# Edge masks from GpSimd to VectorE and the per-node scalar chain from VectorE to GpSimd, in a two-layer graph kernel

## The chip, the cores and the metric

The kernel runs on one core of a Trainium2 chip. Times are device microseconds (us) of one execution. I call the engines as the profile does: PE is TensorE, DVE is VectorE, ACT is ScalarE, POOL is GpSimd. Every kernel ran in turn with the kernel before on the same chip, and its ratio is to that kernel; the experiments used several chips, so two of them are compared by their ratios. A run is called slow when it takes over 1.5% more than the fastest of its kernel; ratios use the other runs, the fast ones.

## The reference, cut to what matters

Two graph layers over 3327 nodes with 64 features and a dense 0/1 adjacency. Layer 0 is an attention in hyperbolic space: a logarithm map for every pair of nodes, a weighted sum over the neighbours, then a chain of per-node steps (a norm, a tanh, a Möbius addition, a projection, a layer norm). Layer 1 weighs each neighbour by 0.5 to the power of its rank from the end of the row.

```python
# layer 0
adj_att = sigmoid(left[:, None] + right[None, :] + b_att[0]) * adj
x_local = logmap(x[:, None, :], x[None, :, :], c)           # every pair
support_t = einsum('ij,ijd->id', adj_att, x_local)
h0 = proj(expmap(x, support_t, c), c)                       # per node: norms, tanh, mobius_add
# ... x = x + h0; layer norm, relu ...
# layer 1
mask = (adj != 0)
rank = cumsum(mask, axis=1); deg = rank[:, -1:]
k = minimum(deg, 100.0);     pos = rank - (deg - k)
w = mask * where(pos > 0, 0.5 ** (k - pos), 0.0)
out = w @ (input @ weight) + bias
```

## The kernel before

The nodes are padded to 26 blocks of 128. The pair stage goes through four strips of columns (8, 8, 6 and 4 blocks wide), with 26, 26, 26 and 13 rounds: a round takes one block of rows (two in the last strip) against the strip. Each round:

- POOL makes an edge mask of the adjacency tile. PE counts edges with it, and ACT or DVE *reads* the count into 8 bits, which layer 1 decodes later.
- PE makes the pair products `pq`. ACT runs two Gelus on them and a tanh for the attention. DVE makes two products: the first with the adjacency, the second with `pq`. PE sums the result.

When a strip has ended, its per-node chain (`post`) is woven into the rounds of the next strip. It is a generator that yields the weight of each portion, and each round takes portions up to a budget. The last strip has no next one: its chain is woven into the decoding of layer 1, which I call the tail.

```python
ON_ACT = ((1, 5), (4, 7), (2, 3), (1, 2))        # share of reads on ACT, by strip
PORTIONS, LAST = (2, 5, 5, 16), 6
BIG, LATER = 4, 99
...
def rsqrt(pool, y, v, n, power=False):
    ...
    if power:
        G.tensor_tensor(y, v, nhalf[:, :n], op=ALU.pow)
        V.tensor_scalar(g, v, -0.5, None, op0=ALU.mult)
        yield LATER
    ...                                          # then Newton steps on DVE
...
def post(agg, b0, nb):
    ...
    A.activation(k, t0, AF.Tanh)
    yield LATER
    V.scalar_tensor_tensor(k, k, absr, rn, op0=ALU.mult, op1=ALU.mult)
    yield 1
    V.tensor_mul(y2, u2, k)
    yield 1
    ...                                          # about 30 more of this kind, 8 columns each
    V.tensor_mul(w, hs, wide(t0, nb))            # 512 columns
    yield BIG
    ...
def edges(n):
    ...
    G.tensor_scalar(*args, 0.0, None, op0=ALU.is_equal)

def read(n, j):
    ...
    rest = none[:, NB - 1 - j : NB - j]
    ...
        A.activation(kept, S.pc[:, : S.F], AF.Relu, bias=rest)
    else:
        V.tensor_scalar(kept, S.pc[:, : S.F], rest, 0.0, op0=ALU.add, op1=ALU.max)

def advance(portions):
    while portions > 0:
        portions -= next(steps, LATER)
...
# inside a round
V.scalar_tensor_tensor(sg, sg, 1.0, ad_of.pop(n)[:, :w], op0=ALU.add, op1=ALU.mult)   # first product
...
if n + 1 < R:
    products(n + 1)
advance(PORTIONS[k])
...
V.scalar_tensor_tensor(sg, pq, WD, sg, op0=ALU.add, op1=ALU.mult)                     # second product
```

Of the kernel before, what the change touches and what calls it, by code (L numbers as in the profile page):

```python
# [34 lines left out]
ON_ACT = ((1, 5), (4, 7), (2, 3), (1, 2))  # L35

PORTIONS, LAST = (2, 5, 5, 16), 6
BIG, LATER = 4, 99
# [403 lines left out]
def fast(ctx, tc, x, adj_t, r, w_att, b_att, weight, bias, out, flag):  # L442
# [35 lines left out]
    G.memset(nhalf, -0.5)  # L478
    ident = const.tile([P, P], F32, name="ident")
# [4 lines left out]

    cb = const.tile([P, P], BF16, name="cb")
    ca = const.tile([P, P], BF16, name="ca")
    G.memset(ca, 1.0)
    G.affine_select(out=cb, in_=ca, compare_op=ALU.is_gt, fill=0.0, base=0,
                    pattern=[[-1, P]], channel_multiplier=1)
    G.affine_select(out=cb, in_=cb, compare_op=ALU.not_equal, fill=-float(MAX_NEIGH), base=0,  # L490
                    pattern=[[-1, P]], channel_multiplier=1)
    G.tensor_sub(ca, ca, cb)

    none_i = const.tile([P, NB], I32, name="none_i")
    none = const.tile([P, NB], F32, name="none")
    G.iota(none_i, pattern=[[-P, NB]], base=MAX_NEIGH - P + 1, channel_multiplier=1)
    G.tensor_copy(none, none_i)
# [6 lines left out]
    def scalar_col(name):  # L504
        return const.tile([P, 1], F32, name=name)

    inv_r, c_c, sqc, absr, maxnorm, c2_c, m2c, negc, zs_c, za_c, f_c = (
        scalar_col(n) for n in ("inv_r", "c_c", "sqc", "absr", "maxnorm", "c2_c", "m2c", "negc", "zs_c", "za_c",
# [3 lines left out]
    def rsqrt(pool, y, v, n, power=False):  # L512

        t = pool.tile([P, n], F32, name="rs_t")
        g = pool.tile([P, n], F32, name="rs_g")
        if power:
            G.tensor_tensor(y, v, nhalf[:, :n], op=ALU.pow)  # L517
            V.tensor_scalar(g, v, -0.5, None, op0=ALU.mult)
            yield LATER
        else:  # L520
            V.tensor_scalar(t.bitcast(I32), v.bitcast(I32), 1, None, op0=ALU.logical_shift_right)
            V.tensor_scalar(y.bitcast(I32), t.bitcast(I32), -1.0, float(0x5F3759DF), op0=ALU.mult, op1=ALU.add)
            V.tensor_scalar(g, v, -0.5, None, op0=ALU.mult)
            yield 3
        for _ in range(1 if power else 3):
            V.tensor_mul(t, y, y)
            yield 1
            V.tensor_mul(t, t, g)
            yield 1
            V.scalar_tensor_tensor(y, t, 1.5, y, op0=ALU.add, op1=ALU.mult)  # L530
            yield 1
# [22 lines left out]
    with tc.tile_pool(name="pre", bufs=1) as pre:  # L554
# [17 lines left out]
        for _ in rsqrt(pre, y, v, NB):  # L572
            pass
# [58 lines left out]
        for _ in rsqrt(pre, yr, x2c, NB):  # L632
            pass
# [44 lines left out]
        V.tensor_scalar(m2c, c_c, -2.0, None, op0=ALU.mult)  # L678

# [40 lines left out]

    def post(agg, b0, nb):

        pool = post_pool
        bs = slice(b0, b0 + nb)

        def small(name):
            return pool.tile([P, nb], F32, name=name)

        def big(name):
            return pool.tile([P, nb, D], F32, name=name)  # L730

        hs, v, xs = h[:, bs], agg[:, :, :D], x_sb[:, bs]
        sa, t0, t1, k, y2, u2, xy, hv, vv, rn = (
            small(n) for n in ("sa", "t0", "t1", "k", "y2", "u2", "xy", "hv", "vv", "rn"))
        u, w, dt = big("u"), big("w"), big("dt")

        A.activation(u, v, AF.Square)
        V.tensor_mul(dt, hs, v)
        yield BIG
        V.tensor_reduce(hv, dt, AX.X, ALU.add)  # L740
        yield BIG
        V.tensor_reduce(vv, u, AX.X, ALU.add)
        yield BIG
        V.scalar_tensor_tensor(sa, hv, m2c, agg[:, :, D], op0=ALU.mult, op1=ALU.add)
        yield 1
        V.tensor_mul(sa, sa, su[:, bs])
        yield 1

        V.tensor_mul(xy, hv, sv[:, bs])
        yield 1  # L750
        V.tensor_mul(t0, sa, x2[:, bs])
        yield 1
        V.tensor_sub(xy, xy, t0)
        yield 1
        V.tensor_mul(u2, vv, sv[:, bs])
        yield 1
        V.tensor_mul(t0, sa, hv)
        yield 1
        V.tensor_sub(u2, u2, t0)
        yield 1  # L760
        V.tensor_mul(u2, u2, sv[:, bs])
        yield 1
        V.tensor_mul(t0, sa, xy)
        yield 1
        V.tensor_sub(u2, u2, t0)
        yield 1
        V.tensor_scalar(u2, u2, 0.0, None, op0=ALU.max)
        yield 1

        V.tensor_scalar(t0, u2, MIN_NORM, None, op0=ALU.max)  # L770
        yield 1
        yield from rsqrt(pool, rn, t0, nb, True)
        V.tensor_mul(t0, t0, rn)
        yield 1
        V.tensor_mul(t0, t0, sk[:, bs])
        yield 1
        A.activation(k, t0, AF.Tanh)
        yield LATER
        V.scalar_tensor_tensor(k, k, absr, rn, op0=ALU.mult, op1=ALU.mult)
        yield 1  # L780

        V.tensor_mul(y2, u2, k)
        yield 1
        V.tensor_mul(y2, y2, k)
        yield 1
        V.tensor_mul(xy, xy, k)
        yield 1
        V.tensor_scalar(xy, xy, m2c, -1.0, op0=ALU.mult, op1=ALU.mult)
        yield 1
        V.tensor_scalar(xy, xy, 1.0, None, op0=ALU.add)  # L790
        yield 1
        V.scalar_tensor_tensor(t0, y2, c_c, xy, op0=ALU.mult, op1=ALU.add)
        yield 1
        V.scalar_tensor_tensor(t1, y2, c2_c, x2[:, bs], op0=ALU.mult, op1=ALU.mult)
        yield 1
        V.tensor_add(t1, t1, xy)
        yield 1
        V.tensor_scalar(t1, t1, MIN_NORM, None, op0=ALU.max)
        yield 1
        V.reciprocal(t1, t1)  # L800
        yield 1
        V.tensor_mul(k, k, bal[:, bs])
        yield 1
        V.tensor_mul(k, k, t1)
        yield 1
        V.tensor_mul(t0, t0, t1)
        yield 1
        V.tensor_mul(t1, k, sa)
        yield 1
        V.tensor_sub(t0, t0, t1)  # L810
        yield 1
        V.tensor_mul(k, k, sv[:, bs])
        yield 1

        V.tensor_mul(y2, t0, x2[:, bs])
        yield 1
        V.tensor_mul(t1, k, hv)
        yield 1
        V.tensor_add(y2, y2, t1)
        yield 1  # L820
        V.tensor_mul(y2, y2, t0)
        yield 1
        V.tensor_mul(hv, hv, t0)
        yield 1
        V.tensor_mul(vv, vv, k)
        yield 1
        V.tensor_add(vv, vv, hv)
        yield 1
        V.tensor_mul(vv, vv, k)
        yield 1  # L830
        V.tensor_add(y2, y2, vv)
        yield 1
        V.tensor_scalar(y2, y2, MIN_NORM, None, op0=ALU.max)
        yield 1

        yield from rsqrt(pool, rn, y2, nb, True)
        V.tensor_scalar(rn, rn, maxnorm, 1.0, op0=ALU.mult, op1=ALU.min)
        yield 1
        V.tensor_mul(t0, t0, rn)
        yield 1  # L840
        V.tensor_mul(k, k, rn)
        yield 1
        V.tensor_mul(w, hs, wide(t0, nb))
        yield BIG
        V.tensor_mul(u, v, wide(k, nb))
        yield BIG
        V.tensor_add(xs, xs, w)
        yield BIG
        V.tensor_add(xs, xs, u)
        yield BIG  # L850

        V.tensor_reduce(t0, xs, AX.X, ALU.add)
        yield BIG
        V.scalar_tensor_tensor(w, wide(t0, nb), -1.0 / D, xs, op0=ALU.mult, op1=ALU.add)
        yield BIG
        A.activation(dt, w, AF.Square)
        yield LATER
        V.tensor_reduce(t0, dt, AX.X, ALU.add)
        yield BIG
        V.tensor_scalar(t0, t0, 1.0 / D, EPS_LN, op0=ALU.mult, op1=ALU.add)  # L860
        yield 1
        yield from rsqrt(pool, rn, t0, nb, True)
        V.tensor_scalar(rn, rn, HS, None, op0=ALU.mult)
        yield 1
        V.scalar_tensor_tensor(w, w, 0.0, wide(rn, nb), op0=ALU.max, op1=ALU.mult)
        yield BIG
        A.copy(s2[:, bs, 0], w)
        yield LATER
        V.tensor_sub(s2[:, bs, 1], w, s2[:, bs, 0])
        yield BIG  # L870
# [69 lines left out]
    def edges(n):  # L940
        mask_of[n] = mask = work.tile([P, FMAX], BF16, name="mask", bufs=3)
        args = mask[:, : span(n)], ad_of[n][:, : span(n)]

        G.tensor_scalar(*args, 0.0, None, op0=ALU.is_equal)  # L944
# [14 lines left out]
    def read(n, j):  # L959
# [4 lines left out]
        rest = none[:, NB - 1 - j : NB - j]  # L964
        i = NB - 1 - j
        if (n < AHEAD and k == 0) or i * num // den != (i + 1) * num // den:
            A.activation(kept, S.pc[:, : S.F], AF.Relu, bias=rest)  # L967
        else:
            V.tensor_scalar(kept, S.pc[:, : S.F], rest, 0.0, op0=ALU.add, op1=ALU.max)  # L969
# [45 lines left out]

    def advance(portions):
        while portions > 0:
            portions -= next(steps, LATER)
# [11 lines left out]
    with tc.manual_schedule(engines=IN_ORDER):  # L1030
        products(0)
        for n in range(R):
# [20 lines left out]
            elif n == 1:  # L1053
                left_to_dram()
            if turned:
# [13 lines left out]
            if n + 1 < R:  # L1069
                products(n + 1)  # L1070
            advance(PORTIONS[k])
# [3 lines left out]
            if ended:  # L1075
                strip_out(k - 1)
            V.scalar_tensor_tensor(sg, pq, WD, sg, op0=ALU.add, op1=ALU.mult)  # L1077
# [13 lines left out]
    with tc.tile_pool(name="l1", bufs=2, reuse_waits="tile") as l1, \  # L1091
# [22 lines left out]
        for j in range(late):  # L1114
            wt = decode(j)
            advance(LAST)
# [88 lines left out]
```

## Time and profile before

The kernel took 458.52 us (median of three runs, 457.63 to 458.9). The first line of the page gives the busy time of each engine, its share of the span, and how many instructions it ran:

```profile
PE 368.4 (81%) x1460; PEld 155.6 (34%) x1460; DVE 393.1 (86%) x660; ACT 369.9 (81%) x399; POOL 289.7 (63%) x137
```

No engine is full over the whole span, so the averages don't name the bound; it has to be read stage by stage. The prediction below does that. Its stages start where the first Gelu of each strip starts; the tail starts 3.7 us after the first Gelu of the last round. GpSimd's masks take 2.8 us each on average, and DVE instructions that meet one are stretched.

### The profile page before, as it was taken

How to read it: one execution, taken by the hardware profiler on the slowest of the kernel's cores; microseconds unless marked ns; L12 is line 12 of the kernel's file. 1: busy time of each engine (PE TensorE's matmuls, PEld its weight loads, DVE VectorE, ACT ScalarE, POOL GpSimd, SP SyncE). 2: the span in 40 equal slices, each digit the busy share in tenths (PEclk: the TensorE clock that was granted, in tenths of full speed). 3: DMA queues.
4: the chain of work that ended last, by engine and by line, in shares of the span. 5: the costliest groups of instructions: out<-in, count | busy, mean ns of one | idle time of the engine just before them, and what ended most of it. 6: DMA issues, size and time to landing. Idle time of an engine off the chain costs nothing.

```text
span 456.4 us, 4831 instructions
## 1 busy us (share of the span) xinstructions
PE 368.4 (81%) x1460; PEld 155.6 (34%) x1460; DVE 393.1 (86%) x660; ACT 369.9 (81%) x399; POOL 289.7 (63%) x137
## 2 busy tenths in 40 slices
PE   0336799999998989879889988698778689678973
PEld 0034233333333323323334444343332232233453
DVE  4893899999999799998999999999889999789821
ACT  1647989999999899887899999779798689577930
POOL 8910699887897697695968787959877541014000
PEclk9997999999998999998999999989899899999987
DMA  7402455545555343444236444336443100000002
GB/s 201 201 12 62 136 157 170 166 141 155 154 194 157 110 130 105 143 130 138 73 102 182 119 123 136 103 106 175 146 124 102 53 1 0 1 0 1 1 21 62
DMA packets 23313, 48.98 MB, mean 107 GB/s; under 512 B 8713, under 2 KB 9169, under 8 KB 23279
## 3 DMA queue, kind: packets, MB, share of 16 engines
q1 hardware_dynamic: 20993, 47.66, 35.0%
q10 hardware_dynamic: 2062, 0.87, 0.9%
q0 software_dynamic: 224, 0.07, 0.3%
q8 instruction: 13, 0.21, 0.2%
q14 instruction: 21, 0.17, 0.1%
HBM read 46.40 MB, written 0.87 MB: 104 GB/s over the span
## 4 chain that ended last, share of the span: by engine, by line
PE 34%; DVE 32%; ACT 20%; issue 7%; DMA 2%; POOL 2%; DVEq 0%; ACTq 0%; POOLq 0%
PE po L993 14%; DVE sg L1077 8%; DVE sg L1058 7%; ACT pq L1048 4%; PE pq L983 4%; ACT wt L1100 4%; ACT sg L976 4%; PE pq L984 4%; PE pc L956 4%; PE pc L955 4%; ACT pq L1049 3%; PE pw L1107 2%; DVE behind_lo L969 2%; DVE behind_hi L969 2%; DMA w_lr<-in_w_att 2%
## 5 line engine op out<-in xcount | busy, mean ns | idle before, releaser
L944 POOL TENSOR_SCALAR mask<-ad 128x1024 bf16<-128x1024 f32 (+1 forms) x91 | 254.5, 2801 | 81.9 <-PE pc L955 57.8
L993 PE MATMUL po<-sg,hw 128*65 128x512 f32 (+1 forms) x364 | 161.7, 568 | 1.6 <-DVE sg L1077 1.3
L1058 DVE SCALAR_TENSOR_TENSOR sg<-sg,ad 128x1024 f32<-128x1024 f32 (+1 forms) x91 | 112.6, 1237 | 6.6 <-ACT sg L976 6.5
L1077 DVE SCALAR_TENSOR_TENSOR sg<-pq,sg 128x1024 f32<-128x1024 f32 (+1 forms) x91 | 103.8, 1141 | 2.7 <-ACT pq L1049 1.5
L1048 ACT ACTIVATE pq<-pq 128x1024 f32<-128x1024 f32 (+1 forms) x91 | 86.7, 952 | 20.3 <-PE pq L984 14.9
L976 ACT ACTIVATE sg<-left_b,right 128x1024 f32<-128x1024 f32 (+2 forms) x104 | 100.5, 980 | 0.0
L1049 ACT ACTIVATE pq<-pq 128x1024 f32<-128x1024 f32 (+1 forms) x91 | 86.2, 947 | 2.9
L955 PE MATMUL pc<-mask,ca 128*128 128x512 bf16 (+1 forms) x175 | 66.5, 380 | 23.4 <-DVE behind_hi L969 8.3
L983 PE MATMUL pq<-iu,ju 71*128 71x512 f16 (+1 forms) x182 | 68.7, 377 | 17.0 <-DVE sg L1077 16.3
L956 PE MATMUL pc<-mask,cb 128*128 128x512 bf16 (+1 forms) x182 | 67.7, 382 | 12.6 <-POOL mask L944 11.1
L993 PEld LDWEIGHTS po<-sg,hw 128*65 128x65 f32 x364 | 49.9, 139 | 72.8 <-issue 56.4
L984 PE MATMUL pq<-iz,jz 128*128 128x512 f16 (+1 forms) x182 | 67.5, 378 | 3.8 <-DMA iz<-jz 3.8
L1107 PE MATMUL pw<-wt,s 128*128 128x512 bf16 (+1 forms) x182 | 40.4, 371 | 10.2 <-ACT wt L1100 7.0
L956 PEld LDWEIGHTS <-cb 128*128 128x128 bf16 x182 | 18.2, 100 | 74.2 <-issue 54.3
L969 DVE TENSOR_SCALAR behind_hi<-pc,none 128x1024 uint8<-128x1024 f32 (+2 forms) x26 | 28.2, 1084 | 6.9 <-PE pc L956 6.7
L969 DVE TENSOR_SCALAR behind_lo<-pc,none 128x1024 uint8<-128x1024 f32 (+2 forms) x26 | 29.0, 1115 | 5.1 <-ACT pq L1049 2.6
L967 ACT ACTIVATE behind_hi<-pc,none 128x1024 uint8<-128x1024 f32 (+2 forms) x26 | 24.6, 945 | 8.0 <-PE pc L956 7.9
L983 PEld LDWEIGHTS <-ju 71*128 71x128 f16 x182 | 18.3, 100 | 36.8 <-DVE sg L1077 18.0
L967 ACT ACTIVATE behind_lo<-pc,none 128x1024 uint8<-128x1024 f32 (+2 forms) x26 | 23.9, 919 | 7.8 <-PE pc L956 7.8
L517 POOL TENSOR_TENSOR rn<-t,nhalf 128x8 f32<-128x8 f32 (+2 forms) x8 | 13.7, 1709 | 25.1 <-DVE t L770 22.4
L984 PEld LDWEIGHTS <-jz 128*128 128x128 f16 x182 | 18.3, 101 | 31.2 <-issue 12.0
L1107 PEld LDWEIGHTS <-s 128*128 128x128 f16 x182 | 17.8, 100 | 30.3 <-issue 11.6
(227 smaller groups left out, 302.7 us busy)
## 6 DMA issues: line engine op xcount, KB each, us to landing
ad<-in_adj_t SPq DMA_DIRECT2D x65, 512.0 KB, 3.6
ad<-in_adj_t SPq DMA_DIRECT2D x26, 384.0 KB, 3.2
out<-o SPq DMA_DIRECT2D x6, 128.0 KB, 1.9
left_b<-left_d SPq DMA_DIRECT2D x1, 512.0 KB, 4.7
x_sb<-in_x ACTq DMA_DIRECT2D x1, 416.0 KB, 5.7
x_sb<-in_x SPq DMA_DIRECT2D x1, 416.0 KB, 5.0
left_b<-left_d SPq DMA_DIRECT2D x1, 384.0 KB, 4.1
iz<-jz ACTq DMA_DIRECT2D x2, 128.0 KB, 2.3
```

The costliest lines, as they stand in the source:

```text
L944: G.tensor_scalar(*args, 0.0, None, op0=ALU.is_equal)
L955: T.matmul(S.pc[:, f0:f1], ca, S.before[:, f0:f1], start=False, stop=True, skip_group_check=True)
L956: T.matmul(S.pc[:, f0:f1], cb, now[:, f0:f1], start=S.first, stop=True, skip_group_check=True)
L969: V.tensor_scalar(kept, S.pc[:, : S.F], rest, 0.0, op0=ALU.add, op1=ALU.max)
L976: A.activation(part(n, sg, j), S.left[:, : S.F], AF.Tanh, bias=right[:, j : j + 1], scale=0.5)
L983: T.matmul(part(n, pq, j, f0, f1), ju[:KB, j, :], S.iu[:, f0:f1], start=True, stop=False)
L984: T.matmul(part(n, pq, j, f0, f1), jz[:, j, :], S.iz[:, f0:f1], start=False, stop=True)
L993: T.matmul(S.po[: D + 1, f0:f1], hw[:, j, :], part(n, sg_of[n], j, f0, f1), start=j == NB - 1, stop=j == 0)
L1048: A.activation(pq, pq, AF.Gelu, scale=-WG / QS)
L1049: A.activation(pq, pq, AF.Gelu, scale=WH)
L1058: V.scalar_tensor_tensor(sg, sg, 1.0, ad_of.pop(n)[:, :w], op0=ALU.add, op1=ALU.mult)
L1077: V.scalar_tensor_tensor(sg, pq, WD, sg, op0=ALU.add, op1=ALU.mult)
```

## The change

The intent is to relieve DVE in strips 1 to 3 and to keep late work out of the way of the next round's products:

1. Masks go to DVE (`not_equal` in place of `is_equal`, with the signs of the counting matrices turned). The bias column `none` goes from both kinds of read.
2. The small instructions of the chain, for the three hidden strips, are recorded and issued on GpSimd in bursts, each followed by some rounds that are left to it (`after(slots)`: 2, 4 and 2 rounds). Roots and the reciprocal become a power and some small steps.
3. The last strip's chain stays on DVE; its roots become bit-shift roots of 11 instructions instead of GpSimd powers.
4. The portions go behind the second product (in the last hidden strip, strip 3, one of two helpings stays ahead of it), and ACT's steps of the chain come one round later.
5. Shares and budgets are set anew.

```diff
-ON_ACT = ((1, 5), (4, 7), (2, 3), (1, 2))
-PORTIONS, LAST = (2, 5, 5, 16), 6
+ON_ACT = ((1, 2), (5, 8), (3, 4), (1, 2))
+PORTIONS, LAST = (2, 4, 4, 8), 8
...
+    class Asked:                       # records calls instead of issuing them
+        ...
+            return lambda *args, **kwargs: self.to.append((getattr(self.engine, name), args, kwargs))
...
+        hidden = b0 + nb < NB
+        W = Asked(G if hidden else V, asked_of_w)
...
+        def after(slots):
+            for do, args, kwargs in asked_of_w:
+                do(*args, **kwargs)
+                if not hidden:
+                    yield 1
+            asked_of_w.clear()
+            if not hidden:
+                pass
+            elif nb > 6:
+                yield from [LATER] * slots
+            else:
+                yield from [LATER] * (slots + slots // 2)
+
+        def root(y, v):
+            ...
+            if hidden:
+                W.tensor_tensor(y, v, nhalf[:, :nb], op=ALU.pow)
+                ...                     # 4 small steps
+            else:
+                rsqrt(W, pool, y, v, nb)
...
+        yield from after(2)
+        yield ACT
         A.activation(k, t0, AF.Tanh)
-        yield LATER
-        V.scalar_tensor_tensor(k, k, absr, rn, op0=ALU.mult, op1=ALU.mult)
-        yield 1
-        ...
+        yield 0
+        scaled(k, k, absr, rn)
+        ...
+        yield from after(4)
         V.tensor_mul(w, hs, wide(t0, nb))
...
-        G.tensor_scalar(*args, 0.0, None, op0=ALU.is_equal)
+        V.tensor_scalar(*args, 0.0, None, op0=ALU.not_equal)
...
-            A.activation(kept, S.pc[:, : S.F], AF.Relu, bias=rest)
+            A.activation(kept, S.pc[:, : S.F], AF.Relu)
...
-            V.tensor_scalar(kept, S.pc[:, : S.F], rest, 0.0, op0=ALU.add, op1=ALU.max)
+            V.tensor_scalar(kept, S.pc[:, : S.F], 0.0, None, op0=ALU.max)
...
+            if hi - lo > 1:             # two blocks a round: the last strip
+                advance(PORTIONS[k])
+            V.scalar_tensor_tensor(sg, pq, WD, sg, op0=ALU.add, op1=ALU.mult)
+            if ended:
+                strip_out(k - 1)
             advance(PORTIONS[k])
...
-            V.scalar_tensor_tensor(sg, pq, WD, sg, op0=ALU.add, op1=ALU.mult)
```

## The prediction

> **What bounds the kernel now.** I first cut the span into stages at the starts of the first Gelu (line 1048) of each strip of nodes, and read the busy time of each engine per stage: head, strip 0 (26 rounds), strip 1 (26 rounds), strip 2 (26 rounds, three quarters as wide), strip 3 (13 rounds), tail (the second layer).
>
> ```profile
> core 0: us, PE busy (x) PEld busy (x) DVE busy (x) ACT busy (x) POOL busy (x), PEclk, DMA share, GB/s
> 0.00:43.00 43.00, 13.64 (x120) 8.64 (x121) 29.55 (x98) 19.55 (x24) 21.91 (x32) 0.94 0.42 126
> 43.00:135.17 92.17, 88.75 (x312) 34.77 (x311) 84.01 (x80) 86.69 (x86) 77.22 (x26) 0.99 0.49 151
> 135.17:242.53 107.36, 95.95 (x321) 35.41 (x320) 100.21 (x137) 95.83 (x100) 80.99 (x32) 0.97 0.43 128
> 242.53:330.55 88.02, 75.23 (x317) 34.31 (x316) 81.84 (x137) 78.49 (x104) 71.71 (x32) 0.96 0.47 132
> 330.55:389.70 59.15, 46.80 (x151) 17.11 (x151) 53.92 (x108) 48.61 (x67) 29.59 (x14) 0.97 0.19 55
> 389.70:456.40 66.70, 48.06 (x244) 25.30 (x242) 43.55 (x103) 40.75 (x21) 8.25 (x4) 0.94 0.06 15
> ```
>
> Strip 0 takes 3.45 us a round and TensorE is nearly full: the chain of waits there is a row of TensorE pieces 3.45 us apart. Strip 1 does the same pair work but takes 107.4 us, because the per-node chain of the finished strip is woven into DVE there. DVE is the fullest engine in strips 1 to 3. Next I read the groups of instructions, for the costs.
>
> ```profile
> L944 POOL TENSOR_SCALAR mask<-ad 128x1024 bf16<-128x1024 f32 (+1 forms) x91 | 254.5, 2801 | 81.9 <-PE pc L955 57.8
> ...
> L1058 DVE SCALAR_TENSOR_TENSOR sg<-sg,ad 128x1024 f32<-128x1024 f32 x65 | 85.4, 1314 | 6.6 <-ACT sg L976 6.5
> L1077 DVE SCALAR_TENSOR_TENSOR sg<-pq,sg 128x1024 f32<-128x1024 f32 x65 | 79.1, 1217 | 2.3 <-ACT pq L1049 1.3
> ...
> L837 DVE TENSOR_SCALAR rn<-rn,maxnorm 128x8 f32<-128x8 f32 (+2 forms) x4 | 2.3, 580 | 0.1
> ...
> L1102 DVE TENSOR_SCALAR wt<-behind_lo 128x3328 uint16<-128x3328 uint8 x7 | 13.2, 1892 | 0.0
> ```
>
> Line 837 works on 8 columns like its neighbours, which take 0.16 us, yet takes 0.58. The timeline of strip 1 shows why: while GpSimd holds a mask, DVE instructions stretch.
>
> ```profile
> 158.86 6.22 POOL L944 TENSOR_SCALAR mask<-ad 128x1024 bf16<-128x1024 f32 x2 [0.69 <-PE pc L955]
> ```
> ```profile
> 159.60 1.00 DVE L757 TENSOR_TENSOR t<-sa,hv 128x8 f32<-128x8 f32 x1
> 160.63 0.17 DVE L759 TENSOR_TENSOR u<-u,t 128x8 f32<-128x8 f32 x1
> 161.20 1.22 DVE L1077 SCALAR_TENSOR_TENSOR sg<-pq,sg 128x1024 f32<-128x1024 f32 x1
> 162.34 2.09 DVE L1058 SCALAR_TENSOR_TENSOR sg<-sg,ad 128x1024 f32<-128x1024 f32 x1
> ```
>
> Last, the waits of ACT: its small steps stand in order between large ones and wait for the DVE chain (here in the tail), and the Gelu waits for products that the late second pair product (line 1077) held back.
>
> ```profile
> ACT pq L1048 <- PE pq L984: 14.9, 25, 3.0
> ...
> ACT k L777 <- DVE t L775: 2.6, 1, 2.6
> ```
>
> **What the Trainium skill says.** "VectorE: DVE Perf Modes", section "The perf-mode tier table": an fp32 tensor_scalar in SBUF runs at two results a cycle (1227 ns for 2048 elements), a two-tensor op at one. The trace agrees in kind: the decode of line 1102 does 3328 elements in 1.89 us, line 1077 does 1024 in 1.22. "SBUF — State Buffer", section "SBUF: two separate sides": DVE and GpSimd share a port pair that whoever comes first locks for a whole instruction. The 2.09 and 1.00 us above agree. "Perfetto Trace Analysis", section "GPSIMD Engine Instruction": GpSimd spans in a profile are unreliable, so I don't rest the small GpSimd ops on them.
>
> **The change part by part.** I use start-to-start times where the timeline has them: line 1058 to its follower 1.13 us, line 1077 1.13, a read on DVE (line 969) 1.20, on ACT the two Gelus and the tanh 3.01 a round and a read (line 967) 1.00 more.
>
> *Masks to DVE.* Estimate from line 1102: 1.89 us less 3328/(2 x 0.96 GHz) = 1.73 leaves 0.16 fixed, so 1024 elements take about 0.69 us, 0.60 start to start; 768 take 0.47. Four are before the loop and fall into DVE's 6.3 us wait there or into the head. In the loop: strip 0 26 x 0.60 = 15.6; strip 1 27 x 0.60 = 16.2; strip 2 27 x 0.47 = 12.7; strip 3 9 x 0.60 = 5.4.
>
> *Blocking by GpSimd goes.* Line 1058: (1.314 - 1.217) x 65 = 6.3, and 2.5 for the narrow form. Eleven small groups (837, 757, 839, 860, 526 and so on), mean less 0.165 times count: 12.0, three quarters of it in strips 1 to 3, so 9. Together about 18 us of DVE time in strips 1 to 3.
>
> *Per-node scalars to GpSimd.* In each of three strips 53 DVE instructions of about 0.17 us go: 27 us in all. In their place bursts of some 20, 45 and 7 GpSimd instructions, whose powers took 1.7 us each; they still lock the ports. I allow 8 us of collisions (estimate: eight active rounds a strip, some 0.3 us each).
>
> *Reads moved.* Strip 0 goes from 6 to 13 reads on ACT: DVE -8.4, ACT +7. Strip 1 about -2, strip 2 about -2 on DVE.
>
> Sums for strips 1 to 3 on DVE: -18 - 27 - 4 + 34 + 8 = -7. So the work on DVE hardly falls; ACT gains 3. The gain has to come from waits and order.
>
> *Portions behind line 1077, ACT's steps later.* Strips 1 to 3 take 254.5 us; ACT's work is 223 and becomes 226, DVE's by direct sum becomes 224 to 229. Before, the delayed line 1077 held back TensorE's products and so ACT. With that gone I expect the fuller of the two plus about 5%: 240 us, or **-14**, split -6 (strip 1), -4.5, -3.5.
>
> *Strip 0.* DVE: 1.13 + 1.13 + 0.60 + half of 1.20 = 3.46 a round; ACT 3.01 + 0.50 = 3.51; TensorE 3.45. All three level, so a little slower: **+2**.
>
> *Head.* Two instructions fewer in each of two root chains, no mask blocking them (0.7 us seen at one of them), but up to four masks on DVE: **0**.
>
> *Tail.* The last strip's chain is not hidden and stays on DVE, with a bit-shift root of 11 instructions in place of a GpSimd power: 63 small ones for 53, +1.8 us before the square. ACT does its steps in order between decodes of 2.88 us. By counting portions (8 a block): tanh after the decode of block 5, square after 13, copy after 15 (before: after 3, 13, 17). DVE reaches the square at about 420.9 instead of 418.8, so ACT, which has run further ahead, waits 6.3 us there, 2.5 for the copy and 1.1 for the tanh: 9.9 for 5.2. ACT's last decode ends the stage, so **+4**.
>
> Sum: 0 + 2 - 14 + 4 = -8, so 450.5. My counting of waits is coarse and the bundle looks tuned as a whole, so I shade it to 448.
>
> **Rivals.** (a) *Balance pays fully*: strips 1 to 3 run at ACT's pace (97, 79 and 49 us) and the tail loses nothing; then about 436. For it: in strip 0 a full engine did run at 97% of the span. (b) *Mask at one element a cycle*, or blocked by the GpSimd bursts: 0.5 us more in 91 rounds on a full DVE, some 40 us, about 480. Against it: line 1102 runs at two. (c) *GpSimd bursts too long for the rounds left to them*: the next large DVE step or ACT's tanh waits for GpSimd, a new wait takes the old one's place, and strips 1 to 3 give 5 instead of 14: about 457. The 1.7 us powers and the lock speak for it, the empty GpSimd against it. (d) *ACT becomes the bound everywhere*, with more reads: 318 of 347 us from the first Gelu to the tail; if it stays idle as long as now (37 us) nothing is gained: 462.
>
> **Range and chances.** The sum gives 450, rival (a) 436, (c) and (d) 457 to 462. I take 448 with 438 to 458. The border of faster by 2% is 449.4, so the chances are near even with more on the good side: faster 0.53, same 0.43, slower 0.04.
>
> **What would show it.** Mask on DVE 0.6 to 0.7 us at 1024; line 1058 back to 1.22 everywhere but in the bursts; strip 0 at 3.5 to 3.6 us a round; strips 1, 2, 3 near 101, 83.5 and 55.5 us with ACT or DVE over 93% busy; the tail longer by about 4 us with ACT waiting for DVE before the square. The prediction is wrong if the mask takes over 1 us, if ACT or DVE waits for GpSimd by more than 5 us in all, if strips 1 to 3 shrink by over 20 us, or if the tail does not grow.

## The result

The changed kernel took 453.15 us (median of four runs, 451.87 to 454.5) against 458.07 us (456.79 to 458.9) for the kernel before in the same rounds. The ratio is 0.9895, with a 95% interval of 0.9853 to 0.9938. A ratio here is the mean time of one kernel's fast runs over that of the other's in the same rounds, so it isn't quite the ratio of the medians. The profiled run was the 454.5 us one, the slowest of the four.

So the time lies inside the predicted range, but the gain is 4.9 us, where 10.5 was predicted.

The first line of the page after the change:

```profile
PE 371.7 (82%) x1438; PEld 159.3 (35%) x1460; DVE 383.3 (85%) x579; ACT 371.5 (82%) x410; POOL 95.7 (21%) x231
```

GpSimd went from 63% to 21% busy, and DVE lost only ten microseconds. The busy times by stage, in the same columns as in the prediction's first fence:

```profile
core 0: us, PE busy (x) PEld busy (x) DVE busy (x) ACT busy (x) POOL busy (x), PEclk, DMA share, GB/s
0.00:44.22 44.22, 14.22 (x120) 9.23 (x121) 29.42 (x101) 19.27 (x25) 6.57 (x26) 0.96 0.42 123
44.22:137.47 93.25, 90.71 (x307) 35.57 (x312) 88.92 (x99) 91.64 (x93) 0.00 (x0) 0.97 0.49 148
137.47:237.99 100.52, 94.00 (x316) 35.84 (x320) 94.44 (x102) 94.98 (x103) 34.77 (x68) 0.97 0.46 137
237.99:325.20 87.21, 76.20 (x313) 36.13 (x316) 76.16 (x102) 77.50 (x106) 29.08 (x68) 0.92 0.46 134
325.20:382.60 57.40, 47.34 (x147) 17.20 (x149) 48.07 (x58) 47.28 (x66) 24.55 (x68) 0.94 0.20 58
382.60:452.80 70.20, 49.20 (x240) 25.34 (x244) 46.25 (x121) 40.85 (x21) 0.73 (x1) 0.91 0.06 14
```

Set against the stages of before:

| stage | before | after | difference | predicted |
|---|---|---|---|---|
| head | 43.0 | 44.2 | +1.2 | 0 |
| strip 0 | 92.2 | 93.3 | +1.1 | +2 |
| strip 1 | 107.4 | 100.5 | -6.8 | -6 |
| strip 2 | 88.0 | 87.2 | -0.8 | -4.5 |
| strip 3 | 59.2 | 57.4 | -1.8 | -3.5 |
| tail | 66.7 | 70.2 | +3.5 | +4 |

Each stage is read from one profiled run. The head is the same code in nine of the experiments, and there it took 43.4 to 44.5 us, so differences of about 1 us are not told apart.

The reader is to see two things. In strips 2 and 3 the gain is nearly missing. And there no engine is full any more: in strip 2 DVE and ACT are busy for 76 and 77 of 87 us, where DVE had 82 of 88 before. Something is waited for.

The groups of instructions answer to the two costs that the prediction made most of, the mask and the stretching of DVE (columns: busy time, mean ns of one, then the idle time before them):

```profile
L1075 DVE SCALAR_TENSOR_TENSOR sg<-sg,ad 128x1024 f32<-128x1024 f32 x65 | 79.0, 1216 | 7.0 <-ACT sg L981 6.7
L1090 DVE SCALAR_TENSOR_TENSOR sg<-pq,sg 128x1024 f32<-128x1024 f32 x65 | 79.0, 1215 | 2.4 <-ACT pq L1065 2.3
...
L950 DVE TENSOR_SCALAR mask<-ad 128x1024 bf16<-128x1024 f32 x65 | 44.4, 684 | 0.0
...
L972 ACT ACTIVATE behind_lo<-pc 128x1024 uint8<-128x1024 f32 x15 | 15.2, 1014 | 2.0 <-PE pc L962 2.0
...
L974 DVE TENSOR_SCALAR behind_lo<-pc 128x1024 uint8<-128x1024 f32 x11 | 13.4, 1215 | 0.8 <-remote 0.8
```

The mask costs 0.684 us. The first product (line 1075 now, 1058 before) is down from 1.314 to 1.216 us, as short as the second. The last two lines are the reads without their bias column. With it, in the kernel before, they were longer:

```profile
L969 DVE TENSOR_SCALAR behind_lo<-pc,none 128x1024 uint8<-128x1024 f32 x16 | 20.5, 1280 | 4.1 <-ACT pq L1049 2.6 <-PE pc L956 1.6
...
L967 ACT ACTIVATE behind_lo<-pc,none 128x1024 uint8<-128x1024 f32 x10 | 11.1, 1106 | 0.5 <-PE pc L956 0.5
```

So the bias that the change drops was worth 0.09 us a read on ACT and 0.065 on DVE. In e4 below, which keeps the bias but has its masks on DVE, such reads still take 1.10 and 1.28 us, so it is not the masks. The prediction didn't price it.

The list of waits (total us, times, longest) names what is new. Line 849 is the first wide step on DVE after the second GpSimd burst, and it needs the result of that burst:

```profile
DVE w L849 <- POOL t L755: 11.2, 3, 4.4
```

One such wait falls in each of the three strips, of 3.2, 3.6 and 4.4 us. The timeline of strip 1 shows how it comes about. These are six instructions of the GpSimd burst (start, duration, operation); it runs from 171.57 to 190.80, so 19.2 us for some 40 instructions on 8 columns:

```profile
171.57 1.03 POOL L755 TENSOR_SCALAR k<-k,absr 128x8 f32<-128x8 f32 x1 [4.77 <-ACT k L809]
...
181.10 0.20 POOL L755 TENSOR_TENSOR k<-k,t 128x8 f32<-128x8 f32 x1
181.26 0.20 POOL L755 TENSOR_TENSOR t<-t,t 128x8 f32<-128x8 f32 x1
181.55 1.12 POOL L755 TENSOR_TENSOR t<-k,sa 128x8 f32<-128x8 f32 x1
...
187.12 1.67 POOL L755 TENSOR_TENSOR rn<-y,nhalf 128x8 f32<-128x8 f32 x1
...
190.60 0.20 POOL L755 TENSOR_TENSOR k<-k,rn 128x8 f32<-128x8 f32 x1
```

And DVE in the same stretch:

```profile
180.26 1.21 DVE L1090 SCALAR_TENSOR_TENSOR sg<-pq,sg 128x1024 f32<-128x1024 f32 x1
181.39 1.21 DVE L1075 SCALAR_TENSOR_TENSOR sg<-sg,ad 128x1024 f32<-128x1024 f32 x1
...
186.25 1.22 DVE L1090 SCALAR_TENSOR_TENSOR sg<-pq,sg 128x1024 f32<-128x1024 f32 x1 [0.17 <-ACT pq L1065]
190.67 0.69 DVE L849 TENSOR_TENSOR w<-h,t 128x512 f32<-128x512 f32 x1 [3.20 <-POOL t L755]
191.28 1.22 DVE L1075 SCALAR_TENSOR_TENSOR sg<-sg,ad 128x1024 f32<-128x1024 f32 x1
```

A small GpSimd instruction takes 0.20 us, and 0.28 from start to start when it depends on the one ahead (0.16 when it doesn't). A power takes 1.67. But the one at 181.55 took 1.12: it met line 1075, which had started at 181.39, and ended just after it. DVE's instruction took its usual 1.21. The two ahead of it, at 181.10 and 181.26, ran under line 1090, whose `pq` lies in PSUM, and kept their 0.20. The trace has this throughout: of the GpSimd instructions of the bursts (powers left out) that started under line 1075, which reads two SBUF tensors, 23 of 24 took 0.5 us or more, and each ended only after line 1075 had; of 71 that started under line 1090, 69 stayed under 0.35. So the contention for the shared ports that the prediction cites is at work, with GpSimd as the one that waits.

At 187.47 DVE was ready for the burst's result, 15.9 us after the burst had begun; the burst took 19.2. While DVE waits in its order, the next round's first product waits too. That round of strip 1 took 6.6 us; a typical one takes 3.0 or 3.9.

In strips 2 and 3 the bursts took 16.2 and 15.5 us, and DVE was ready for them after 12.4 and 11.1. In strip 3 the wide step stands ahead of the second product, so that product was held up as well, and the round took 10.4 us instead of 3.75.

How much of this is stretching? In the three second bursts, the instructions over 0.3 us, powers aside, took 6.8, 3.1 and 3.9 us more than at 0.20 each. Without that the bursts would have lasted about 12.4, 13.1 and 11.6 us, with 15.9, 12.4 and 11.1 left for them (an estimate from the profile's GpSimd durations, which are rough). By this estimate most of the wait is stretching. No run tried a burst that avoids line 1075.

The waits also reach TensorE: it stood still for 2.4, 3.2 and 5.3 us around them, and its granted clock then read 0.50 for 3.6, 7.0 and 7.2 us.

In the tail, ACT waits as the prediction has it (the stage's own list of waits):

```profile
ACT dt L863 <- DVE w L860: 5.8, 1, 5.8
...
ACT s L874 <- DVE w L871: 2.3, 1, 2.3
ACT k L809 <- DVE t L755: 0.7, 1, 0.7
```

The view of the chain that ended last came out empty for this kernel, so the page gives no shares by line to set against those of before.

### The profile page after: what moved, and what is told of

Its sections match the earlier page's. It is cut to its first block, busy times and chain, and to the rows that moved or that the text cites. A ratio compares the mean times of both kernels' runs of the same rounds, so it can differ in the third digit from the quotient of the medians.

```text
span 452.8 us, 4738 instructions
## 1 busy us (share of the span) xinstructions
PE 371.7 (82%) x1438; PEld 159.3 (35%) x1460; DVE 383.3 (85%) x579; ACT 371.5 (82%) x410; POOL 95.7 (21%) x231
## 4 chain that ended last, share of the span: by engine, by line
## 5 line engine op out<-in xcount | busy, mean ns | idle before, releaser
L998 PE MATMUL po<-sg,hw 128*65 128x512 f32 (+1 forms) x364 | 164.2, 576 | 1.6 <-DVE sg L1090 1.5
L1075 DVE SCALAR_TENSOR_TENSOR sg<-sg,ad 128x1024 f32<-128x1024 f32 (+1 forms) x91 | 103.7, 1139 | 7.0 <-ACT sg L981 6.7
L981 ACT ACTIVATE sg<-left_b,right 128x1024 f32<-128x1024 f32 (+2 forms) x104 | 100.5, 980 | 0.0
L961 PE MATMUL pc<-mask,ca 128*128 128x512 bf16 (+1 forms) x169 | 64.8, 383 | 24.4 <-DVE behind_lo L974 11.7
L962 PE MATMUL pc<-mask,cb 128*128 128x512 bf16 (+1 forms) x170 | 63.9, 385 | 15.9 <-DVE mask L950 13.9
L950 DVE TENSOR_SCALAR mask<-ad 128x1024 bf16<-128x1024 f32 (+1 forms) x91 | 59.2, 652 | 0.6 <-PE pc L961 0.6
L755 POOL TENSOR_SCALAR sa<-hv,m2c 128x8 f32<-128x8 f32 (+1 forms) x3 | 3.0, 1004 | 201.5 <-ACT behind_hi L972 147.9
L972 ACT ACTIVATE behind_lo<-pc 128x1024 uint8<-128x1024 f32 (+2 forms) x32 | 27.4, 855 | 12.2 <-PE pc L962 6.8
L972 ACT ACTIVATE behind_hi<-pc 128x1024 uint8<-128x1024 f32 (+2 forms) x31 | 27.0, 871 | 8.1 <-PE pc L962 8.1
L961 PEld LDWEIGHTS <-ca 128*128 128x128 bf16 x175 | 17.9, 102 | 30.6 <-issue 19.5
L1132 POOL TENSOR_TENSOR x_sb<-x_sb,bias_b 128x256 f32<-128x256 f32 (+1 forms) x7 | 7.2, 1042 | 79.5 <-DVE w L860 79.5
```

The source lines that it names most:

```text
L950: V.tensor_scalar(*args, 0.0, None, op0=ALU.not_equal)
L961: T.matmul(S.pc[:, f0:f1], ca, S.before[:, f0:f1], start=False, stop=True, skip_group_check=True)
L962: T.matmul(S.pc[:, f0:f1], cb, now[:, f0:f1], start=S.first, stop=True, skip_group_check=True)
L981: A.activation(part(n, sg, j), S.left[:, : S.F], AF.Tanh, bias=right[:, j : j + 1], scale=0.5)
L998: T.matmul(S.po[: D + 1, f0:f1], hw[:, j, :], part(n, sg_of[n], j, f0, f1), start=j == NB - 1, stop=j == 0)
```

## The experiments

Twelve kernels ran, each correct against the reference. The theory: the gain of strips 1 to 3 is cut short by the waits for GpSimd's second burst (A). Its rivals: the masks overfill DVE, or the turn from strip to strip costs the gain (C). Other runs take the parts of the change one by one.

### More rounds for the second burst: e1_slots

```diff
-        yield from after(4)
+        yield from after(6, 8)
-        def after(slots):
+        def after(slots, narrow=None):
-                yield from [LATER] * (slots + slots // 2)
+                yield from [LATER] * (narrow or slots + slots // 2)
```

> The changed kernel with more rounds between the second GpSimd burst and the DVE step that reads it (6 in place of 4 rounds, 8 in place of 6 half rounds in the last strip). In the changed kernel DVE waits 3.2, 3.6 and 4.4 us there (11.2 us) and the rounds around are up to 6.6 us longer. Theory A (these waits are on the path and are where the expected gain went): the three waits vanish and the time falls by 7 to 11 us, to about 443 to 446. Rival B (ACT or the transitions bound the strips and only hide these waits): under 3 us, 450 to 453.

It took 442.54 us (438.89 to 443.49; ratio to before 0.9634, 0.959 to 0.9679), 10.6 us less than the median of the changed kernel (2.6% by the ratios). The waits all but went:

```profile
DVE w L849 <- POOL t L755: 1.3, 1, 1.3
```

and the strips shrank, here strips 1, 2 and 3 in the view by stage:

```profile
core 0: us, PE busy (x) PEld busy (x) DVE busy (x) ACT busy (x) POOL busy (x), PEclk, DMA share, GB/s
...
136.93:235.85 98.92, 94.86 (x318) 36.06 (x322) 94.27 (x101) 94.66 (x103) 34.70 (x68) 0.97 0.48 142
235.85:317.10 81.25, 72.35 (x313) 34.29 (x315) 74.74 (x100) 77.28 (x106) 31.04 (x68) 0.98 0.50 142
317.10:369.60 52.50, 45.84 (x147) 16.59 (x148) 48.40 (x57) 46.81 (x66) 25.21 (x68) 0.97 0.22 62
```

GpSimd does as much as in the changed kernel, but nothing stands behind it. Strips 1 to 3 take 232.7 us, 12.5 less than after the change and 21.9 less than before. ACT is now 96% busy in strip 1 and 95% in strip 2. The place fits, too. From first Gelu to first Gelu, the three rounds with the waits took 6.6, 6.5 and 10.4 us after the change, and take 3.9, 3.1 and 3.7 here: some 13 us less, against 12.5 for strips 1 to 3 as a whole. The three stretches of half clock that followed the waits are gone. A is shown: two more rounds of patience (one in strip 3) were the missing half of the gain.

### The turn from strip to strip later: e2_turn_late

The transposes of a finished strip were moved behind the next round's products.

```diff
-            if turned:
-                pa = turn(k - 1)
-            elif n > 1:
+            if n > 1 and not turned:
                 total(n - 2)
...
                 products(n + 1)
+            if turned:
+                pa = turn(k - 1)
```

> The changed kernel with the turn of the finished strip's sums on TensorE put behind the products of that round, not ahead of the counts. In the changed kernel TensorE idles 2.3 us (strip 1) and 2.5 us (strip 2) before the turn and then runs matmuls at 0.63 us instead of 0.38 for a few us; two long rounds follow at each of three transitions, 10.5 us in excess. Theory C (the transition is a second place where the gain went): the idle goes and the time falls by 3 to 6 us. Rival: ACT waits for the turn later instead, within 2 us of the changed kernel.

453.03 us (ratio 0.988, 0.984 to 0.992): no gain over the change. The reason to try was this stretch of the changed kernel in strip 2, on PE:

```profile
242.41 0.27 PE L989 MATMUL pq<-iz,jz 128*128 128x256 f16 x1
245.23 1.10 PE L1010 MATMUL po<-ident,sg 65*128 65x65 f32 x8 [2.54 <-DVE sg L1004]
246.55 0.63 PE L962 MATMUL pc<-mask,cb 128*128 128x512 bf16 x1 [0.22 <-PE po L1010]
```

PE stands still for 2.54 us, and its matmuls then take 0.63 us instead of 0.38 until 252. In the profile with the late turn, strips 1 and 2 were 2.6 us shorter each, strip 3 was 0.5 longer (its transition rounds took 5.7, 8.1 and 4.6 us, for 4.5, 5.0 and 3.7) and the tail 1.6 longer. But that was one of the two fastest of the six runs (450.71 us), and the profile of the change its slowest, so the profiles show a gain that the medians don't. C is not confirmed as a cause of the missing gain.

### Masks alone: e4_masks_alone

The kernel before, with its masks on DVE and the new shares of reads, and nothing else.

```diff
-        G.tensor_scalar(*args, 0.0, None, op0=ALU.is_equal)
+        V.tensor_scalar(*args, 0.0, None, op0=ALU.is_equal)
-ON_ACT = ((1, 5), (4, 7), (2, 3), (1, 2))
+ON_ACT = ((1, 2), (5, 8), (3, 4), (1, 2))
```

> The kernel before with only the masks moved to DVE and the new shares of reads on ACT. DVE gains 34 us of masks in strips 1 to 3 and loses about 18 us of blocking and 4 us of reads. Theory (by the sums of the prediction DVE is the bound there): slower than before by 4 to 10 us, 462 to 468. Rival (GpSimd's blocking and the late masks were what held the kernel before): faster, 448 to 454, as the whole change.

456.71 us (ratio 0.9967, 0.993 to 1.0003): a miss, it is not slower. The masks cost DVE 59 us (44.4 + 14.9), and yet strips 1 to 3 fell from 254.5 to 250.3 us:

```profile
core 0: us, PE busy (x) PEld busy (x) DVE busy (x) ACT busy (x) POOL busy (x), PEclk, DMA share, GB/s
...
137.50:240.74 103.24, 92.48 (x315) 34.07 (x319) 102.07 (x161) 96.72 (x102) 6.36 (x5) 1.00 0.45 133
240.74:327.01 86.27, 73.91 (x313) 33.84 (x316) 83.72 (x161) 79.14 (x106) 7.15 (x5) 0.98 0.48 137
327.01:387.80 60.79, 47.16 (x148) 17.16 (x151) 57.11 (x117) 48.79 (x67) 5.12 (x5) 0.97 0.18 52
```

DVE is now full, 99% of strip 1 and 97% of strip 2. But its busy time in these strips only rose from 236.0 to 242.9. Some 34 us of masks were added there by the prediction's count (from start to start; the durations add up to more, since DVE instructions overlap by 0.08 us or so), so some 27 us went. About 4 of these are reads moved to ACT, which leaves some 23 us that DVE had lost to GpSimd's masks (an estimate). Adding up durations agrees: in strips 1 to 3 line 1058 takes 8 us less than in the kernel before, the small steps of the chain 12 less and the wide ones 2 less, 22 in all. The prediction had 18. DVE is overfilled, but that this makes the kernel slower than before is refuted.

### The chain back on DVE: e7_chain_on_dve

The changed kernel with the small steps on DVE again, roots by GpSimd powers in all strips.

```diff
-        hidden = b0 + nb < NB
+        hidden = False
-PORTIONS, LAST = (2, 4, 4, 8), 8
+PORTIONS, LAST = (2, 5, 5, 8), 8
...                                     # and the roots of e3_tail_pow
```

> The changed kernel with the whole per-node chain on DVE again (the roots' power on GpSimd as before), in portions of 5, behind the second product. It tells what the move to GpSimd is worth. Theory (DVE is the bound, the move saves some 27 us of DVE but gives 11 us of waits back): slower than the changed kernel by 2 to 8 us, 455 to 461, and far slower than the version with more slots (442.5). Rival (ACT is the bound, DVE had room): equal to or faster than the changed kernel, 445 to 453.

455.14 us (ratio 0.9919, 0.9879 to 0.9958), not told apart from the change (0.9895). Its strips 1 to 3:

```profile
136.95:240.69 103.74, 94.83 (x320) 34.68 (x319) 101.39 (x154) 95.35 (x102) 10.46 (x5) 0.98 0.44 131
240.69:327.01 86.32, 74.55 (x317) 34.04 (x316) 82.78 (x154) 77.78 (x106) 9.22 (x5) 0.98 0.48 137
327.01:385.30 58.29, 48.67 (x151) 17.50 (x151) 55.28 (x110) 47.82 (x67) 6.04 (x5) 0.94 0.20 56
```

DVE is full again (98% of strip 1). The move to GpSimd frees 7 us of DVE a strip, 20.8 in all (from 239.5 to 218.7). But e7 also has the last strip's roots of e3, which are worth up to 3 us by themselves, so its like is e3 (on another chip) and not the change: 0.9816 for 0.9919. As shipped the move buys about 1%, since much of the freed time goes into waiting. With e1's patience it buys 3.7% (e10, which has those roots too and ran beside e7: 0.9555 for 0.9919).

### Masks back on GpSimd: e8_masks_on_pool

```diff
-        V.tensor_scalar(*args, 0.0, None, op0=ALU.not_equal)
+        G.tensor_scalar(*args, 0.0, None, op0=ALU.is_gt)
-ON_ACT = ((1, 2), (5, 8), (3, 4), (1, 2))
+ON_ACT = ((1, 5), (4, 7), (2, 3), (1, 2))
```

For an adjacency of zeros and ones the two comparisons agree.

> The changed kernel with the masks on GpSimd again (and the old shares of reads), so that bursts and masks share it. Theory (the masks had to leave for the bursts to fit): a mask emitted behind a burst of 16 to 19 us comes late, the counts and ACT wait for it at nine places, 465 us or more. Rival (GpSimd was idle 36% and takes both): 450 to 456.

485.16 us (ratio 1.0541, 1.0487 to 1.0595). Its profile fell on a slow run (489.89 us), so I take from it only the kind of wait, not a size to compare. PE waits for masks that stand behind a burst:

```profile
PE pc L962 <- POOL mask L950: 50.2, 12, 11.2
```

So the two moves belong together: with bursts on GpSimd, the masks have to leave it.

### The order of the portions: e5_portions_first, e11_slots_portions_first

The portions ahead of the second product again, in the changed kernel and in e1_slots.

```diff
             if hi - lo > 1:
                 advance(PORTIONS[k])
+            advance(PORTIONS[k])
             V.scalar_tensor_tensor(sg, pq, WD, sg, op0=ALU.add, op1=ALU.mult)
...
-            advance(PORTIONS[k])
```

> The changed kernel with its portions put back ahead of the second pair product, all else as changed. Theory (order pays: a late second product holds back TensorE's products and then ACT; before, those waits were 16 us on TensorE and 15 us on ACT): slower than the changed kernel by 3 to 8 us, 456 to 461. Rival (the order is worth nothing once the chain is off DVE): within 2 us of 453.

> More slots (442.5 us), with the portions put back ahead of the second product. Without the waits for GpSimd this shows the order alone. Theory (the order pays): 3 us or more slower, 445.5 to 449. Rival (it is worth nothing, as it was in the changed kernel): 441 to 444.

e5: 455.43 us, ratio 0.9902 (0.985 to 0.9954), against 0.9895 for the change. e11: 442.45 us, ratio 0.9667 (0.9635 to 0.9699), against 0.9634 for e1. The profile of e5 does show the waits that the order was to remove (DVE 15.0 us for the bursts, ACT 14.1 for products), but neither pair of times is told apart. The new order is not shown to be worth anything: with the waits gone the two ratios differ by 0.3%, less than the width of either interval.

### ACT's steps in the same round: e6_act_at_once

```diff
             portion = next(steps, LATER)
-            asked = portion == ACT
+            if portion == ACT:
+                next(steps)
             portions -= portion
```

> The changed kernel with ACT's steps of the per-node chain in the round in which they come up, not one round later. Theory (the delay keeps ACT from waiting for DVE): ACT waits for DVE or GpSimd in order, 1 to 2 us at each of nine steps less what it gains, slower by 1 to 4 us. Rival (the delay lengthens the chain and nothing else): the second burst starts earlier, DVE's three waits of 11 us shrink, faster by 1 to 3 us.

451.26 us (448.46 to 452.53; ratio 0.9828, 0.9783 to 0.9873). The delay is not shown to help; if anything the kernel is faster without it. Here DVE's waits for the bursts were 8.7 us instead of 11.2: the second burst started 0.5, 3.1 and 2.0 us earlier in its strip.

### The last strip's roots by GpSimd powers: e3_tail_pow

```diff
-                rsqrt(W, pool, y, v, nb)
+                Asked(G, asked_of_w).tensor_tensor(y, v, nhalf[:, :nb], op=ALU.pow)
+                W.tensor_mul(t, y, y)
+                W.scalar_tensor_tensor(t, v, -0.5, t, op0=ALU.mult, op1=ALU.mult)
+                W.scalar_tensor_tensor(y, t, 1.5, y, op0=ALU.add, op1=ALU.mult)
```

> The changed kernel with the last strip's three roots as before (a power on GpSimd and three DVE instructions in place of eleven DVE instructions). Theory D (the tail is longer because ACT waits for the longer DVE chain, 5.8 us before the square and 2.3 before the copy): DVE reaches the square 2.5 us earlier, the tail shrinks by 3 to 4 us, the time to about 449.5. Rival: the powers' 2 us stand in the chain and eat it, no change.

450.02 us (448.35 to 452.15; ratio 0.9816, 0.978 to 0.9852), 3.1 us below the change. Counted from the first decode, ACT's last decode ends at 46.84 us instead of 48.61 (44.83 before). The same 1.8 us lie between e1 (48.63) and e10 (46.83), so a power and three small steps do let ACT through earlier than eleven small steps. But the 1.8 us did not reach the end of these two profiles: from the first decode to the end both took about 67 us (66.9 and 67.0), as the stretch after the last decode ran at a granted clock of 0.79 instead of 0.83. The profile of e3 was 2.2 us ahead before the first decode, where the two kernels do the same. So where the 3 us come from is not located, and the intervals of 0.9816 and 0.9895 all but touch.

### Together: e10_slots_tail, e9_all, e12_head_masks

e10 is e1 and e3. e9 adds the late turn of e2. e12 is e10 with the masks of the rounds before the loop on GpSimd, since the head had grown by 1.2 us.

```diff
+        if n > AHEAD:
             V.tensor_scalar(*args, 0.0, None, op0=ALU.not_equal)
+        else:
+            G.tensor_scalar(*args, 0.0, None, op0=ALU.is_gt)
```

> More slots (-10.6 us measured alone) and the tail's roots on GpSimd (-3.1 measured alone) together. If they lie in different stages they add: 438.5 to 440.5 us. If the tail only moves its wait, 442.

> More slots and the tail's roots on GpSimd (439.2), with the turn of a finished strip put behind the products. The transitions cost some 10 us in excess. If TensorE's idle time of 5.8 us before the turns is on the path: 434 to 437. If ACT is the bound, 438 to 440; over 441 if the chain, one round later, no longer fits its strip.

> More slots and the tail's roots on GpSimd (439.2), with the four masks of the head on GpSimd as before. The head became 1.2 us longer with them on DVE. If those masks are the reason, 438.0; if not, 439 or more.

e10: 439.24 us (436.42 to 440.7), ratio 0.9555 (0.9519 to 0.9592): the two gains add. e9: 444.01 us, ratio 0.97 (0.9669 to 0.9732), 1.5% worse than e10, a miss: the late turn does harm, with strip 3 transition rounds of 5.9, 7.9 and 4.6 us (4.7, 6.6 and 3.7 in e10). e12: 437.09 us, ratio 0.9552 (0.9505 to 0.9599), the same as e10's. Its head is 42.5 us long in the profile instead of 43.5, but the times don't show the microsecond. e10 and e12 beat both kernels, by 4.5% and some 3.4% (0.9555 over 0.9895).

## Why the prediction was right or wrong

**Right, in kind and size.** The mask costs 0.684 us at 1024 columns, as worked out. Line 1058's stretching went. Strip 0 runs at 3.46 us a round (3.91 and 3.02 in turn; ACT is 98% busy) and is 1.1 us longer, for +2. The tail grew by 3.5, for 4, with ACT's three waits at 5.8, 2.3 and 0.7, for 6.3, 2.5 and 1.1. Strip 1 gave 6.8 us, for 6, but this is luck: the reason given for it failed, and a wait of 3.2 us took part of a gain that is 8.4 us in e1.

**Wrong: the step "Per-node scalars to GpSimd".** It allowed "8 us of collisions" and put them on DVE. None are seen there: line 1075 takes 1.216 us on average over all its executions, those in the bursts among them, and line 1090 1.215. The collisions lengthened GpSimd's instructions. The step counted the instructions of a burst (45, where the trace has 39) but never worked out how long one takes, nor how long DVE leaves it. The burst took 15.5 to 19.2 us where 11.1 to 15.9 were left, and DVE waited 11.2 us in all. The prediction set that as its own sign of being wrong ("more than 5 us in all"), and told it as rival (c), "a new wait takes the old one's place". The mechanism of that rival came true: the wait cost 10.6 us of time, as e1 shows, and the rival had priced it at 9 (5 instead of 14). The strips still gave 9.4 us and not 5, as they had more to give. The rival was given too little weight: the prediction left the small GpSimd instructions unpriced because of the page's caution on GpSimd spans. The trace of before could have priced the powers, some 3 of the burst's 19 us; it had no burst to read the rest from.

**Misread: the lock.** The prediction says that the 2.09 and 1.00 us of its timeline agree with a lock for a whole instruction. They show contention, but not that: line 757 ended 1.71 us, and line 1058 0.65 us, before the mask that it had met. And line 1077, with one operand in PSUM, ran its usual 1.22 us inside a mask in the same lines. Which DVE line a GpSimd instruction meets decides whether it is stretched, and the prediction's flat 0.3 us a round doesn't ask that.

**Wrong in the other direction.** "The fuller of the two plus about 5%" gave 240 us for strips 1 to 3. Two terms of it were off:

- The sums were too high. DVE came to 218.7 us and ACT to 219.8, where 224 to 229 and 226 were predicted. On DVE some 23 us of blocking went with the masks by e4, not 18, and the chain with its collisions took off another 24 (from e4 to the change, about 2 of them the bias), where 27 less 8 were predicted. On ACT it was, for the most part, the bias column, which wasn't priced: some 0.09 us in each of the 47 reads of these strips, so 4 of the 6 us.
- The surplus of 5% held only where nothing waits for GpSimd. In e1 strips 1 to 3 take 232.7 us for 218.8 of ACT, a surplus of 6%; in the changed kernel 245.1 for 219.8, one of 11.5%.

Without the missing wait the right sums would have given some 231 us, near what e1 reaches. So the potential of the change lay between the predicted 240 and the 225 of rival (a), "balance pays fully", and the wait took half of it. That the sums were too high hid part of the wait, so it is partly luck that 453 lies within the range.

**Wrong: the reason given for the -14.** It was laid to the order, portions behind line 1077 and ACT's steps later. e5, e11 and e6 show no gain from either. What the strips gain comes from DVE: the masks take away the stretching (e4, e7: DVE is 98 to 99% full in strip 1 and the kernel is still not slower than before), and the chain on GpSimd then takes 21 us off it (e7 against the change).

**Small ones.** The head grew by 1.2 us in the profile, not 0. With masks on DVE there, the heads of the experiments took 43.2 us (e4) to 44.5, and with them back on GpSimd 42.5 (e12); that the masks are the reason is likely but no time shows it. And the last step, shading 450.5 to 448 because the bundle looked tuned, went the wrong way: the sum as it stood was nearer.

**Open.** Where the gain of e3 lies; why a late turn shortens strips 1 and 2 and lengthens strip 3; and what the new shares and budgets are worth by themselves, which no run tried alone.

## What to carry to other kernels

When work moves to an engine that has nothing to do, work out how long a burst takes there, stretched by the lock, and how long its reader will take to get to it: an engine with time to spare can still be late. Give the result more rounds than it needs, because in a hidden chain a later result costs nothing as long as the strip has rounds left: in e1 strips 1 to 3 only got shorter. And price the operand that a change drops along with the instructions that it moves: here, on ACT in strips 1 to 3, it gave back the 4 us that the moved reads cost.

## What the Trainium skill lacked or had wrong

- "SBUF — State Buffer", section "SBUF: two separate sides", says that whoever starts first holds the shared port pair for the whole instruction and that the other fully blocks. For DVE instructions with one tensor input that met a GpSimd mask in the kernel before, this fits: 8 of the 9 small ones that were stretched ended with the mask (to 0.03 us). All 12 small ones with two tensor inputs got through earlier, 1.7 us before the end of a 1024-column mask and 1.3 us before that of a 768-column one, by the profile's spans. In the other direction, with GpSimd instructions of 0.20 us against DVE's of 1.2 us, DVE shows no loss (1.216 us on average) and GpSimd's stretch to about 1.1 us.
- "GPSIMD Engine Reference", section "3.1 Elementwise — side-by-side cycle accounting", has no figure for GpSimd's cost of one small instruction; its measured times are for 512 and 2048 elements. Here, on 8 columns: 0.20 us, 0.28 from start to start when dependent and 0.16 when not, 1.67 for a power (1.35 on 6 columns), and 15.5 to 19.2 us for a burst of 39.
- "TensorE: Matmul & The Clock Gate", section "What's actually happening", has the clock halve after an idle window of about 3.4 us. In strip 2 of the changed kernel 2.54 us of idleness were enough: the granted clock was 0.50 from 245 to 252 us, and a matmul of 0.38 us took 0.63. Not every such pause does it: in the kernel before TensorE stood still for 2.56 us at 402 us and the granted clock stayed at 1.
- I found on no page what a per-partition scalar column costs DVE in reading PSUM. Dropping it took 1024-column reads from 1280 to 1215 ns.
